# A 128-column stationary operand in one column stage of a four-layer convolution kernel on one Trainium2 core

## The chip, the cores and the metric

The kernel runs on one core of a Trainium2 chip. The metric is device time in microseconds (us) of one execution, everything on the chip included. An engine is named as in the profile: PE is TensorE (matmul), PEld its weight load, DVE is VectorE, ACT ScalarE, POOL GpSimd, and SP the queue that issues the DMAs.

## The reference, cut to what matters

Four layers act on `x` of shape (4, 64, 256, 256) in fp32. Layers 0, 2 and 3 are long convolutions; layer 1 goes to a Haar basis, mixes channels there, shrinks, and goes back.

```python
x = conv(x, L0)          # per channel: rows and columns convolved with a separable filter
f1 = haar2d(x)           # L1
acc = sum(soft_threshold(einsum('bchw,oc->bohw', f1 * v[i], conv_w[i]), tau[i]) for i in range(2))
x = haar2d(acc, inverse=True) + x
x = conv(x, L2)
x = conv(x, L3)

def conv(x, w):          # hx, hy: small sine networks of z, times a decay
    k = einsum('ijk,imk->ijmk', hx, hy)
    y = irfft2(rfft2(x, s=(512, 512)) * rfft2(k, s=(512, 512)) / 512)[..., :256, :256]
    return y + x * bias[:, None, None]
```

Since the filter of a channel is an outer product of two sequences, a convolution is a causal 256 by 256 Toeplitz product along the columns of an image and one along its rows.

## The kernel before, in words

**Tiles.** The four batches make two groups of two. A group has 32 rounds, and a round takes two channels of the two batches, so four images of 256 by 256. In SBUF the partition is (batch, 64 rows) and the free axis is (channel, block of 64 rows, column). There are 64 rounds, called t in the code; `alone` is 32, so t below 32 is the first group.

**Phases.** Phase A (t over all rounds) does layer 0 and the forward Haar. Phase B, once for each group, does the channel mix and the shrink in units: one unit is a matmul group `mix` (L607, four matmuls of 512 columns into the PSUM tile f), a multiply, subtract and threshold on DVE (L626, L646, L651), sign and magnitude on ACT, and additions on POOL (L669, L670). Phase C does the inverse Haar and layers 2 and 3.

**Phase C.** A round is 18 pieces, written out by hand in `piece`: four pieces of `rows` of layer 2 for t (PSUM tile c1r), a half of the inverse Haar product (c0ps, L308), four pieces of `columns` of layer 3 for t - 2 (c2c), four of `rows` of layer 3 for t - 1 (c2r), the other half of the Haar product, and four of `columns` of layer 2 for t (c1c). What a piece hands to ACT or DVE is queued with `later` and issued at the start of the next piece by `flush`. So each engine's order is fixed in the program.

**The Toeplitz product.** One piece is one j, a block of 64 output positions: `toeplitz` (the matmuls are L296) goes over four blocks k and, for each, over the four 64 by 64 tiles (r, c) of the PE array. The stationary operand is 64 by 64 of the data, the moving operand is the filter, 256 - 64k columns wide. A fp32 matmul is two passes, each with a weight load and a matmul in the profile. In the row stage r is the batch and c the channel; the result in PSUM has the channel on its partition half. ACT copies it to the SBUF tile `ch` (L861), after which a partition half is a channel. In the column stage r is the channel and c the batch; the filter, `filters_y(toep)`, depends on r alone. DVE adds the residual out of PSUM (`residual`, L880), into o for layer 3.

**What runs beside what.** `beside` interleaves lists of pieces by count. The mix of the second group (`phase_b(1)`) is spread over the first 29 rounds of phase C:

```python
cut_a, cut_c = (ROUNDS + 2) * A_PIECES + BLOCKS + 4, (ROUNDS - AHEAD) * C_PIECES
...
beside(main, phase_b(1), len(a_end) - 1 + 2 * BLOCKS, 0)
...
beside(c[cut_c:], [], 0, 0)
```

These rounds are called the shared stretch here; after them phase C runs by itself, the lone stretch. The column stage of layer 3 for t = 0 to 26 lies in the shared stretch, for t = 27 to 31 (and all of the second group) in the lone one.

Of the kernel before, what the change touches and what calls it, by code (L numbers as in the profile page):

```python
# [48 lines left out]
B, C, N = 4, 64, 256  # L49

ROW = 64
BLOCKS = N // ROW
# [46 lines left out]
def conv_haar_kernel(  # L99
    ctx: ExitStack, tc: tile.TileContext, x, zT, w1, wbd, cols, wo, decay, wo_first, decay_first, bias, forward, inverse, wrow, pack, v, v_rows, out  # L100
):
    nc = tc.nc
# [21 lines left out]
    def big(tag, name, bufs):  # L124
        return ac.tile([P, 2 * M, N], F32, tag=tag, name=name, bufs=bufs)

    def blocks(images):

        return images.rearrange("p (i k) j -> p i k j", i=2)
# [4 lines left out]
    def banks(name):  # L134

        ring = rings[asked[0] % len(rings)]
        asked[0] += 1
        return [ring.tile([P, 2, N], F32, tag="ps", name=f"{name}_{r}") for r in range(2)]
# [150 lines left out]
    def half(r):  # L289
        return slice(r * ROW, (r + 1) * ROW)  # L290

    def toeplitz(ps, data, t, j):

        for k in range(BLOCKS):
            for r, c in TILES:
                nc.tensor.matmul(  # L296
                    ps[r][half(c), j % 2, k * ROW :],
                    data[half(r), c, k, bass.ts(j, ROW)],
                    t(r, c)[:, : N - k * ROW],
                    start=k == 0,  # L300
                    stop=k == BLOCKS - 1,
                    tile_position=(r * ROW, c * ROW),
                )

    def haar(ps, pairs, matrix):

        for r, c in TILES:
            nc.tensor.matmul(  # L308
                ps[r][half(c)].rearrange("p h k -> p (h k)"),
                matrix[half(r)],  # L310
                pairs(r, c).rearrange("p h k -> p (h k)"),
                start=True,
                stop=True,
                tile_position=(r * ROW, c * ROW),
            )

    def filters_x(toep):
        return lambda r, c: toep[half(r), c * PERIOD : c * PERIOD + N]

    def filters_y(toep):  # L320
        return lambda r, c: toep[half(r), CI * PERIOD :]
# [72 lines left out]
    def later(op):  # L394

        waiting.append(op)
# [23 lines left out]
    def phase_a():  # L420
# [13 lines left out]
        def rows(t, j):  # L434
            s = st[t]
            if j == 0:
                s["y"] = big("t0", f"ay_{t}", 2)
            if j % 2 == 0:
                s["ps"] = banks(f"a1ps{j}_{t}")
            toeplitz(s["ps"], blocks(s["x"]), filters_x(s["toep"]), j)  # L440
            if j % 2:
                for r, ps in enumerate(s["ps"]):
                    y = blocks(s["y"])[:, r, j - 1 : j + 1]
                    later(lambda y=y, ps=ps: nc.scalar.copy(y, ps))  # L444

        def columns(t, j):
            s = st[t]
            if j == 0:
                s["x1"] = big("m0", f"x1_{t}", 2)
            if j % 2 == 0:  # L450
                s["ps2"] = banks(f"a2ps{j}_{t}")
            toeplitz(s["ps2"], blocks(s["y"]), filters_y(s["toep"]), j)
            if j % 2:
                for e, ps in enumerate(s["ps2"]):
                    later(lambda e=e, ps=ps: residual(t, e, j, ps))
            if j == BLOCKS - 1:
                s["fw"] = big("m1", f"fw_{t}", 2)
                s["ops"] = forward_free(s["x1"], s["fw"], f"f{t}_")
# [281 lines left out]
    def phase_c():  # L740
# [3 lines left out]
        alone = total - ROUNDS  # L744
# [3 lines left out]
        def load(t, k=slice(0, 4)):  # L748
            if t >= total:
                return  # L750
            if t < 2:
                g = bp.tile([P, 2, 2, W], F32, tag="v", name=f"g_{t}", bufs=3)
                st[t]["g"] = g.rearrange("p i k w -> p (i k w)").rearrange("p (n k) -> p n k", k=N)
            elif k.start == 0:
                st[t]["g"] = big("in", f"g_{t}", 3)
                st[t]["scales"] = scales(st[t]["g"])
            for rows, g in all_rows(mixed[t // ROUNDS], t % ROUNDS, st[t]["g"], False)[k]:
                nc.sync.dma_start(g, rows)

        def load_raw(t):  # L760
            if alone <= t < total:
                r = st[t]["raw"] = late["sb"].tile([P, 2 * M, N], F32, tag="raw", name=f"raw_{t}", bufs=2)
                for rows, to in all_rows(unshrunk, t % ROUNDS, r, False):
                    nc.sync.dma_start(to, rows)
# [71 lines left out]
        def product(t, h):  # L836
# [9 lines left out]
            for e, ps in enumerate(two):  # L846
                z = blocks(s["y"])[:, e, 2 * h : 2 * h + 2]
                copy = nc.vector.tensor_copy if e and t >= alone else nc.scalar.copy
                later(lambda z=z, ps=ps, copy=copy: copy(z, ps))

        def rows(t, l, j):
            s = st[t]
            if j == 0:
                s["half", l] = big("t0", f"ch{l}_{t}", 2)
            if j % 2 == 0:
                s["ps", l] = banks(f"c{l}r{j}_{t}")
            toeplitz(s["ps", l], blocks(s["y"]), filters_x(s["toep", l]), j)
            if j % 2:
                for r, ps in enumerate(s["ps", l]):
                    y = blocks(s["half", l])[:, r, j - 1 : j + 1]  # L860
                    later(lambda y=y, ps=ps: nc.scalar.copy(y, ps))  # L861

        def columns(t, l, j):
            s = st[t]
            if j == 0:
                s["new"] = big("out", f"o_{t}", 2) if l == 2 else big("m0", f"cy_{t}", 2)
            if j % 2 == 0:
                s["ps", l] = banks(f"c{l}c{j}_{t}")
            toeplitz(s["ps", l], blocks(s["half", l]), filters_y(s["toep", l]), j)
            if j % 2:  # L870
                new, old = blocks(s["new"]), blocks(s["y"])
                for e, ps in enumerate(s["ps", l]):
                    later(lambda e=e, ps=ps: residual(t, l, e, j, new, old, ps))
            if j == BLOCKS - 1:
                s["y"] = s["new"]

        def residual(t, l, e, j, new, old, ps):
            at = l * C + t % ROUNDS * CI + e
            to, of = new[:, e, j - 1 : j + 1], old[:, e, j - 1 : j + 1]
            nc.vector.scalar_tensor_tensor(to, of, bias_sb[:, at : at + 1], ps, ALU.mult, ALU.add)  # L880
            if l == 2 and t == total - 1:

                nc.sync.dma_start(blocks(out[t // ROUNDS, t % ROUNDS])[:, e, j - 1 : j + 1], to)
# [13 lines left out]
        def piece(t, j):  # L897
# [28 lines left out]
            if R1 <= j < R1 + BLOCKS:  # L926
                if t < total:
                    rows(t, 1, j - R1)
            elif C2 <= j < C2 + BLOCKS:
                if 1 < t:  # L930
                    columns(t - 2, 2, j - C2)
            elif R2 <= j < R2 + BLOCKS:
                if 0 < t <= total:
                    rows(t - 1, 2, j - R2)
            elif j >= C1:
                if t < total:
                    columns(t, 1, j - C1)
            else:
                product(t + 1, int(j > BLOCKS))
# [35 lines left out]

    late = {}
    (a, a_last, a_end), (c_before, c_first, c) = phase_a(), phase_c()

    cut_a, cut_c = (ROUNDS + 2) * A_PIECES + BLOCKS + 4, (ROUNDS - AHEAD) * C_PIECES
# [150 lines left out]
```

## Time and profile before

| | |
|---|---|
| median of 6 runs | 2567.8 us (2562.58 to 2578.39) |
| the profiled execution's own time | 2568.21 us |
| its span, first to last instruction | 2565.5 us |
| mean granted PE clock | 0.979 |
| PE busy | 2320.4 us (90%) |
| PEld busy | 1880.6 us (73%) |
| POOL busy | 2068.3 us (81%) |
| DVE busy | 1830.5 us (71%) |
| ACT busy | 1324.6 us (52%) |
| matmul group of the last column stage, c2c (L296) | 8192 passes, 319.1 us busy, 299 ns mean of one |
| first and last c2c matmul | 1169.4 us, 2561.0 us |

Times inside the span are counted from its first instruction. The end of a matmul is modelled, and it includes the time that results take to leave the array, so matmuls that follow each other overlap in the records, and a busy PE is not a PE at its peak. A matmul group's busy time counts overlapping ones once. A wait is put down to the instruction whose semaphore came last; "issue" means that the engine waited for nothing that the profile shows.

### The profile page before, as it was taken

The page shows a single profiled execution, that of the slowest core. Times are in us where ns is not written, and L with a number is a line of the kernel's source. Part 1 is how long each engine was busy: PE and PEld are TensorE (multiplying, and loading weights), DVE is VectorE, ACT ScalarE, POOL GpSimd, SP SyncE. Part 2 cuts the span into 40 slices and gives each one's busy share as a digit, 9 for nine tenths or more (in the row PEclk, how much of TensorE's full clock was granted, in tenths as well). Part 3 has the DMA queues.
Part 4 walks back from the last instruction along what each step waited for, and adds up shares of the span by engine and source line. Part 5 has one row for each costly group of instructions (what it writes and reads, how often), then busy time and mean ns, then how long its engine had stood idle before and what let it go on. Part 6 is the DMA issues. An engine that isn't in the chain of part 4 may idle for free.

```text
span 2565.5 us, 118462 instructions
## 1 busy us (share of the span) xinstructions
PE 2320.4 (90%) x53292; PEld 1880.6 (73%) x53292; DVE 1830.5 (71%) x2049; ACT 1324.6 (52%) x2187; POOL 2068.3 (81%) x2428
## 2 busy tenths in 40 slices
PE   5999998788888888878999999999989999999999
PEld 4877887445444444646777887777789999999998
DVE  2555545799999999856767676766757777777763
ACT  1221112566666666325666666666655555555552
POOL 1898887899989999768767777776879999999991
PEclk8999999899999999978999999999999999999999
DMA  7676998699999999656989898988876666666653
GB/s 211 223 246 229 295 310 294 249 346 319 339 341 314 351 322 328 239 194 207 325 306 315 310 327 308 310 308 300 293 224 220 216 209 221 215 212 215 219 163 110
DMA packets 203676, 685.23 MB, mean 267 GB/s; under 512 B 29289, under 2 KB 30826, under 8 KB 190755
## 3 DMA queue, kind: packets, MB, share of 16 engines
q1 hardware_dynamic: 203171, 677.67, 77.4%
q8 instruction: 418, 6.85, 1.1%
q14 instruction: 87, 0.71, 0.1%
HBM read 427.93 MB, written 249.63 MB: 264 GB/s over the span
## 4 chain that ended last, share of the span: by engine, by line
PE 47%; DVE 4%; issue 2%; DMA 1%; POOL 1%; ACT 1%; SPq 0%; DVEq 0%; ACTq 0%; POOLq 0%
PE c2c L296 10%; PE c2r L296 10%; PE c1r L296 10%; PE c1c L296 9%; PE f L607 4%; PE c0ps L308 4%; DVE cy L880 1%; DVE m L651 1%; DVE x L626 1%; DVE x L646 1%; DMA ft<-coef 0%; POOL i L385 0%; DMA toep<-filt 0%; DMA rows<-in_v_rows 0%; ACT ch L861 0%
## 5 line engine op out<-in xcount | busy, mean ns | idle before, releaser
L385 POOL TENSOR_TENSOR i<-i,g 128x16 f32<-128x16 f32 x744 | 431.6, 600 | 27.2
L296 PEld LDWEIGHTS a2ps<-toep,ay 64*64 64x64 f32 x8192 | 306.4, 137 | 146.8 <-DVE f L477 71.8
L607 PE MATMUL f<-ft,mix 64*64 64x512 f32 x2048 | 301.9, 620 | 110.7 <-DVE x L626 89.5
L296 PE MATMUL a2ps<-toep,ay 64*64 64x128 f32 (+3 forms) x8192 | 356.6, 307 | 33.3 <-DVE f L477 28.5
L296 PEld LDWEIGHTS a1ps<-toep,x 64*64 64x64 f32 x8192 | 288.4, 134 | 87.8 <-issue 45.9
L296 PE MATMUL a1ps<-toep,x 64*64 64x128 f32 (+3 forms) x8192 | 336.3, 299 | 16.2 <-DMA x<-in_x 9.9
L296 PEld LDWEIGHTS c2c<-toep,ch 64*64 64x64 f32 x8192 | 311.9, 134 | 46.6 <-issue 17.2
L296 PEld LDWEIGHTS c1c<-toep,ch 64*64 64x64 f32 x8192 | 302.3, 133 | 47.0 <-issue 20.1
L296 PE MATMUL c1r<-toep,z 64*64 64x256 f32 (+3 forms) x8192 | 320.4, 299 | 12.8 <-issue 8.5
L296 PEld LDWEIGHTS c1r<-toep,z 64*64 64x64 f32 x8192 | 299.5, 134 | 42.4 <-issue 25.4
L296 PE MATMUL c2c<-toep,ch 64*64 64x128 f32 (+3 forms) x8192 | 319.1, 299 | 8.1 <-ACT ch L861 5.4
L385 POOL TENSOR_TENSOR ci<-i,g 128x1024 f32<-128x1024 f32 x124 | 317.3, 2579 | 4.5
L296 PEld LDWEIGHTS c2r<-toep,cy 64*64 64x64 f32 x8192 | 296.8, 134 | 32.3 <-issue 21.3
L296 PE MATMUL c2r<-toep,cy 64*64 64x128 f32 (+3 forms) x8192 | 314.0, 298 | 6.0 <-issue 4.4
L669 POOL TENSOR_TENSOR gt<-m,ft 128x512 f32<-128x512 f32 x128 | 163.3, 1276 | 193.2 <-DVE m L651 189.7
L296 PE MATMUL c1c<-toep,ch 64*64 64x256 f32 (+3 forms) x8192 | 311.8, 297 | 4.8 <-issue 3.5
L444 ACT COPY ay<-a1ps 128x512 f32<-128x512 f32 x256 | 137.3, 589 | 346.0 <-PE a1ps L296 345.4
L632 ACT ACTIVATE m<-x 128x1024 f32<-128x1024 f32 x194 | 206.0, 1062 | 210.2 <-DVE x L626 102.2
L861 ACT COPY ch<-c2r 128x512 f32<-128x512 f32 x256 | 137.3, 590 | 291.2 <-PE c2r L296 290.5
L477 DVE TENSOR_TENSOR f<-a3ps,wrow_sb 128x512 f32<-128x512 f32 x256 | 161.3, 681 | 132.9 <-PE a3ps L308 132.9
L626 DVE TENSOR_TENSOR x<-f,v 128x1024 f32<-128x1024 f32 x192 | 233.1, 1214 | 20.5 <-PE f L607 19.4
L880 DVE SCALAR_TENSOR_TENSOR o<-cy,bias_sb,c2c 128x512 f32<-128x512 f32 x256 | 176.7, 740 | 95.4 <-PE c2c L296 94.9
(84 smaller groups left out, 3941.3 us busy)
## 6 DMA issues: line engine op xcount, KB each, us to landing
toep<-filt SPq DMA_DIRECT2D x384, 224.0 KB, 5.1
ft<-coef SPq DMA_DIRECT2D x128, 512.0 KB, 7.9
v<-in_v SPq DMA_DIRECT2D x64, 1024.0 KB, 9.1
mixed<-gt SPq DMA_DIRECT2D x128, 512.0 KB, 6.9
g<-mixed SPq DMA_DIRECT2D x256, 256.0 KB, 5.0
x<-in_x SPq DMA_DIRECT2D x128, 256.0 KB, 4.4
coef<-f SPq DMA_DIRECT2D x128, 256.0 KB, 3.8
x<-in_x SPq DMA_DIRECT2D x32, 1024.0 KB, 8.1
```

The lines of the kernel that those rows point to most:

```text
L296: nc.tensor.matmul(ps[r][half(c), j % 2, k * ROW :], data[half(r), c, k, bass.ts(j, ROW)], t(r, c)[:, : N - k * ROW], start=k == 0, stop=k ...
L308: nc.tensor.matmul(ps[r][half(c)].rearrange("p h k -> p (h k)"), matrix[half(r)], pairs(r, c).rearrange("p h k -> p (h k)"), start=True, s ...
L385: engine.tensor_tensor(to, s, d, op)
L444: later(lambda y=y, ps=ps: nc.scalar.copy(y, ps))
L477: later(lambda f=f, ps=ps, w=w: nc.vector.tensor_tensor(f, ps, w, ALU.mult))
L607: nc.tensor.matmul(un[u]["f4"][half(q), b, :], mixers[0][half(r), bass.ts(i, C)], st[s]["f"][half(r), b], start=True, stop=True, tile_posi ...
L626: nc.vector.tensor_tensor(un[u]["x"], un[u]["f4"], both(u, "v"), ALU.mult)
L632: nc.scalar.activation(un[u]["m"], un[u]["x"], AF.Sign)
L646: nc.vector.tensor_tensor(un[u]["a"], un[u]["a"], both(u, "tau"), ALU.subtract)
L669: nc.gpsimd.tensor_tensor(g[:, 0], m[:, 0], st[s]["f"][:, 0], ALU.add)
L861: later(lambda y=y, ps=ps: nc.scalar.copy(y, ps))
L880: nc.vector.scalar_tensor_tensor(to, of, bias_sb[:, at : at + 1], ps, ALU.mult, ALU.add)
```

## The change

In the column stage of layer 3 for the first group, `wide(t, l)`, the two images of one channel (the two batches) are multiplied in one stationary operand of 64 partitions by 128 columns, on the 64 by 128 half r of the array, instead of two operands of 64 by 64. So that the 128 columns lie next to each other, ACT writes the row results `ch` in the order (k, j, image, 64) instead of (image, k, 256); `turn` does it, in as many copies as before. Each j has 8 matmuls instead of 16, with moving operands of the same widths. In the built program the PE has 1024 c2c matmuls of 64 by 128 in place of 2048 of 64 by 64, out of 4096; the orders of ACT, DVE, POOL and SP stay as they were, but for the shape of 128 copies. `mix` pieces and the other stages keep 64 by 64 tiles, so the wide matmuls stand in 54 unbroken runs, 49 in the shared stretch and 5 in the lone one.

```diff
+    def side_by_side(data):
+
+        return data.rearrange("p n k -> p (n k)").rearrange("p (k j c q) -> p k j c q", k=BLOCKS, j=BLOCKS, c=2)
+
+    def toeplitz_wide(ps, data, t, j):
+
+        for k in range(BLOCKS):
+            for r in range(2):
+                nc.tensor.matmul(
+                    ps[r][:, j % 2, k * ROW :],
+                    data[half(r), k, j].rearrange("p c q -> p (c q)"),
+                    t(r, 0)[:, : N - k * ROW],
+                    start=k == 0,
+                    stop=k == BLOCKS - 1,
+                    tile_position=(r * ROW, 0),
+                )
+
+    def turn(data, r, j, ps):
+
+        to = side_by_side(data)[:, j - 1 : j + 1, :, r]
+        nc.scalar.copy(to, ps.rearrange("p i (j q) -> p i j q", q=ROW))
...
+        def wide(t, l):
+            return t < alone and l == 2
+
         def rows(t, l, j):
...
                 for r, ps in enumerate(s["ps", l]):
+                    if wide(t, l):
+                        later(lambda r=r, ps=ps: turn(s["half", l], r, j, ps))
+                        continue
                     y = blocks(s["half", l])[:, r, j - 1 : j + 1]
                     later(lambda y=y, ps=ps: nc.scalar.copy(y, ps))
...
-            toeplitz(s["ps", l], blocks(s["half", l]), filters_y(s["toep", l]), j)
+            if wide(t, l):
+                toeplitz_wide(s["ps", l], side_by_side(s["half", l]), filters_y(s["toep", l]), j)
+            else:
+                toeplitz(s["ps", l], blocks(s["half", l]), filters_y(s["toep", l]), j)
```

## The prediction

> **What bounds the kernel now.** The page's chain comes first: it tells whose time the end is made of. PE leads by far, and its part is spread evenly over the six Toeplitz stages, c2c with a tenth.
>
> ```profile
> PE 47%; DVE 4%; issue 2%; DMA 1%; POOL 1%; ACT 1%; SPq 0%; DVEq 0%; ACTq 0%; POOLq 0%
> ```
>
> Then the two stretches in which the changed stage runs, by windows cut at starts of c2c stages: 25 rounds of the shared stretch, 20 of the lone one. The columns are length, busy time of each engine with its records, PE clock, DMA share and GB/s.
>
> ```profile
> core 0: us, PE busy (x) PEld busy (x) DVE busy (x) ACT busy (x) POOL busy (x), PEclk, DMA share, GB/s
> 1206.50:1851.20 644.70, 607.08 (x14152) 499.58 (x14148) 453.26 (x434) 405.64 (x709) 465.57 (x519) 1.00 0.90 312
> 1918.90:2303.30 384.40, 384.28 (x10568) 368.71 (x10563) 283.39 (x320) 224.30 (x421) 362.38 (x361) 1.00 0.67 215
> ```
>
> In the lone stretch PE never stops: 384.40 / 20 = 19.2 us a round. In the shared one a round takes 644.7 / 25 = 25.8 us, PE is busy for 94%, and DVE, ACT and POOL for 63 to 72%. So PE sets the pace in both, and what the change does to PE counts. How near it is to its peak shows in one row for each width of the moving operand, here in the lone stretch (busy, then mean ns of one):
>
> ```profile
> L296 PE MATMUL c2c<-toep,ch 64*64 64x256 f32 x160 | 17.4, 377 | 0.0
> L296 PE MATMUL c2c<-toep,ch 64*64 64x192 f32 x160 | 15.2, 323 | 0.0
> L296 PE MATMUL c2c<-toep,ch 64*64 64x128 f32 x160 | 13.1, 269 | 0.0
> L296 PE MATMUL c2c<-toep,ch 64*64 64x64 f32 x160 | 11.0, 217 | 0.0
> ```
>
> Sixty-four columns more cost 53 ns (377 - 323, and so on down), so a pass streams 1.2 columns per ns, and 217 - 53 = 164 ns of each record is the way out of the array. A j has two passes at each of the four widths on each tile: 2 x (213 + 160 + 107 + 53) = 1.07 us if the four tiles stream side by side. Four stages of four j give 17.1 us, and two Haar products (512 columns, two passes: 0.85 each) 1.7, together 18.8 of the 19.2 us. The array is full with 64 by 64 tiles. The wide form has half the matmuls on half the tiles, so it streams for the same 1.07 us; it has nothing to win in the stream, and the question is what comes between the streams.
>
> **Part 1, weight loads.** A load of 64 columns against one of 128, from the c2c loads and from the network's product in phase A (min/median/max):
>
> ```profile
> L296 PEld LDWEIGHTS c2c<-toep,ch x640: 130/133/136, 2206.9 to 2288.6; 64*64 64x64 f32 x160
> L195 PEld LDWEIGHTS mlp_ps<-h,wbd_sb x4: 186/190/190, 98.8 to 99.3; 128*128 128x128 f32 x4
> ```
>
> The difference is 190 - 133 = 57, about 54 ns for 64 columns: a load takes its columns at 1.2 per ns too, 53 and 107 ns. In the records a tile's next load begins as its present matmul begins and runs below it, so a pass costs the longer of its stream and the next load. With 53 ns that hides below every width; 107 ns stands out by 53 ns below the 64-column passes, two in each j. That is 107 ns for a j, 4 x 32 = 128 of them: 13.7 us. In each of the 54 runs the last such pass has no wide load behind it: less 54 x 0.053 = 2.9. Part 1 costs 10.8 us, 9.0 in the shared stretch and 1.8 in the lone one.
>
> The Trainium skill (TensorE: Matmul & The Clock Gate, What overlaps and what doesn't) says that a weight load overlaps running matmuls only in other row groups. By that rule each of the 32 loads of a row half in a stage would stand bare, 32 x 32 x 0.107 = 110 us in all, by estimate; the product at 98.8 us, with all 128 rows in use, contradicts it, since its loads of 107 ns lie below streams of 213 ns and add nothing.
>
> **Part 2, changing the shape of the tile.** Before, phase C has one shape. Afterwards each run is entered and left. The nearest rows are in phase A, where a 128 by 128 product stands between 64 by 64 ones:
>
> ```profile
> 98.65 0.22 PE L296 MATMUL a2ps<-toep,ay 64*64 64x64 f32 x1
> 98.79 0.73 PEld L195 LDWEIGHTS mlp_ps<-h,wbd_sb 128*128 128x128 f32 x4
> 98.79 1.13 PE L195 MATMUL mlp_ps<-h,wbd_sb 128*128 128x256 f32 x4
> 99.85 0.45 PE L296 MATMUL a1ps<-toep,x 64*64 64x256 f32 x4
> ```
>
> The last narrow stream ends at 98.65 + 0.05 = 98.70, and the first load of the new shape starts only at 98.79: 94 ns in which nothing may begin, and then 107 ns of load. Four streams of 0.213 end at 99.75; the next load comes at 99.85, again 94 ns on, with 53 ns to fill. In and out cost 0.20 + 0.15 = 0.35 us. The other changes of shape in phase A (into and out of mlp_out, of 128 rows by 64 columns) show 90 to 97 ns as well. 54 runs x 0.35 = 18.9 us: 17.1 shared, 1.8 lone. All of these rows also change the number of rows, 64 to 128; the new change, 64 by 64 to 64 by 128, alters only the columns. So the bounds are 0 and 18.9 us (and 2 more, since the four tiles end up to 57 ns apart and wait for the last). I take 18.9, as every change of shape in the trace shows it.
>
> The Trainium skill (TensorEngine Tiling (Array Packing), Key Properties) states that a change of tiling mode, not of tile alone, drains the engine, and lists 64 by 64 and 64 by 128 as different configurations: by that rule the upper bound holds, without it the sum below would be about zero.
>
> **Part 3, fewer instructions.** PE's unexplained idle time in the shared stretch (us in total, times, longest):
>
> ```profile
> PE c1r L296 <- issue: 7.0, 10, 1.7
> PE c2r L296 <- issue: 4.4, 5, 1.4
> PE c1c L296 <- issue: 3.5, 5, 1.5
> PE f L607 <- issue: 2.9, 4, 1.1
> PE c2c L296 <- issue: 2.5, 3, 1.9
> ```
>
> With c0ps (0.3) it is 20.6 us in 28 stops, or 25 from the end of the streams (28 x 0.164 more). Number the PE and PEld records in order of time, and these stops begin at numbers that leave 193 or 194 over 256. The page has the partner:
>
> ```profile
> q8 instruction: 418, 6.85, 1.1%
> ```
>
> The 53292 matmul and 53918 load records over 418 packets are 256 a packet: PE waits for its next packet of instructions, in the stretch where the DMA share is 0.90. The lone stretch, at 0.67, has no such stop. The shared window has 28300 records, 110 packets, so 0.23 us a packet. The change takes 256 records out of each of 27 rounds, one packet: 27 x 0.23 = 6.2 us. The packet that lies in the wide stage also lasts up to twice as long, which gives the fetch time; I take half of another 6.2. Relief 9 us; bounds 0 and 25.
>
> The Trainium skill (Runtime: NRT & Kernel Launch, Instruction fetch mechanics) calls the crossing of such a block mostly hidden. By that rule the relief would be nothing and the sum 9 us higher; the 25 us above speak against it for this stretch.
>
> **Part 4, what absorbs it.** Other stops of PE in the shared stretch are mostly mix waiting for DVE to free its PSUM tile (9.4 us) and shape no steady limit; a longer c2c shortens some: 3 us (0 to 6). At the start of the lone stretch PE waits on the rows' DMA anyway, so t = 27 is free: 0.7 us. The ACT copies keep size and place in the order, 588 ns each; they write 64 elements at a time, which no row prices, but ACT is busy 63% of the shared stretch, and `ch` is read most of a round later. At nothing then; if each took half as long again, 128 x 0.29 = 38 us of ACT work would spread over 670 us with 37% idle. No wait, DMA or queue place is added on any engine.
>
> **Sum.** 10.8 + 18.9 - 9 - 3 - 0.7 = 17 us on the profiled execution's 2568.2, which is 0.4 above the median: 2585 us. With all bounds for slower (no relief, nothing absorbed, 2 us for uneven ends) it is + 32; with no drain, + 13.7 - 9 - 3.7 = + 1.
>
> **Rivals.** *No measurable change.* Either only the row split counts for the drain, which gives 2569, or the relief is nearer 20 than 9, which gives 2574. For it: no row shows this very change of shape, and the stops feed back on pace. Against: 94 ns in every change that is shown. *Faster.* The missing packet lets the fetch run ahead, so that all 25 us of stops go, and there is no drain: 13.7 - 25 = - 11, with the 6 us of other waits - 17, so 2551 us. It decides where the relief passes the sum of parts 1 and 2; if part 2 holds, at 30 us, it can't be reached. *Much slower.* The two row halves don't stream side by side in this shape; then a stage takes 4.27 us longer, 32 x 4.27 = 137 us, and with 9 us of relief the time is near 2695. Against: in the 64 by 64 shape the same two halves do run together; no row has two wide tiles. (The Trainium skill, TensorE: Matmul & The Clock Gate, Measured speedup vs the span model, has four row tiles at 3.07 times one; no run here shows it.) That the change isn't made is excluded: the built program has 1024 matmuls of 64 by 128.
>
> **How the numbers follow.** Forecast (slower by 13 to 32 us) 0.57, much slower 0.08, no measurable change 0.25, faster 0.10. About 0.5%, 12.8 us, is what a measurement of this kernel can tell. Slower is 0.57 + 0.08. The likeliest case alone spans 2581 to 2600. The range goes down to 2566 to take in the undrained case, and up to 2601; it leaves out faster, much slower, and a little beyond the bounds.
>
> **What would show it.** In the profile after: a c2c load of about 187 ns, 64 columns; the first load of a wide run 94 ns after the last stream; a j of 1.17 us inside a run; in the lone stretch 20.0 us a round for t = 28 to 31 against 19.2; fewer "issue" stops in the shared stretch. Streams of the two halves that alternate, or a run entered without a gap, would prove it wrong.

## The result, and the profile after

The changed kernel takes 2578.83 us (median of 23 runs, 2573.41 to 2587.25) against 2570.7 us for the kernel before, run beside it (53 runs). The ratio is 1.0033, 95% interval 1.0023 to 1.0043: about 8.5 us slower, clear of the noise, and half of the 17 us that the sum gave. The time lies in the stated range, but below the likeliest case (13 to 32 us slower), and 8.5 us is less than the 12.8 us (0.5%) that the prediction took for the least that can be told; with this many runs it can be told.

The profiled execution has a span of 2578.1 us, 12.6 more than the one before. Of these, 7.3 us have passed when the first c2c matmul starts, before any wide matmul. They are put down to the spread between executions: in the profiles of all kernels below the first c2c load starts between 1168.9 and 1175.1 us without wide stages and between 1167.4 and 1179.3 us with them. The rest follows from the starts of the c2c stages. The 25 shared rounds between the same two stages take 648.1 us against 644.6, so 3.5 more; the kernel that is wide in all rounds, which has the same program in this stretch, takes 647.2, so a difference of 1 us between single profiles means nothing. The rounds t = 29 to 31 of the lone stretch take 59.7 us against 57.6, so 2.1 more for three; the remainder of the kernel is the same to 0.3 us.

The windows of the changed kernel, shared and lone:

```profile
core 0: us, PE busy (x) PEld busy (x) DVE busy (x) ACT busy (x) POOL busy (x), PEclk, DMA share, GB/s
1213.90:1862.00 648.10, 622.28 (x12550) 476.41 (x12546) 457.38 (x434) 405.78 (x709) 463.35 (x519) 0.99 0.89 310
1930.30:1990.00 59.70, 59.70 (x1396) 49.86 (x1396) 44.06 (x48) 33.78 (x64) 54.34 (x55) 1.00 0.64 206
```

The same three lone rounds of the kernel before:

```profile
1918.90:1976.50 57.60, 57.60 (x1592) 55.12 (x1588) 42.84 (x48) 33.97 (x64) 54.81 (x55) 1.00 0.65 211
```

The shared stretch has 12550 + 12546 matmul and load records in place of 28300, so 128 fewer in each of 25 rounds. One lone round is 0.7 us longer (59.7 / 3 = 19.9 us). The wide stage itself, t = 30, by the width of the moving operand (busy, mean), with all wide loads of the run below (min/median/max):

```profile
L313 PE MATMUL c2c<-toep,ch 64*128 64x256 f32 x16 | 2.7, 410 | 0.0
L313 PE MATMUL c2c<-toep,ch 64*128 64x192 f32 x16 | 2.0, 322 | 0.0
L313 PE MATMUL c2c<-toep,ch 64*128 64x128 f32 x16 | 1.6, 271 | 0.0
L313 PE MATMUL c2c<-toep,ch 64*128 64x64 f32 x14 | 1.2, 241 | 0.0
L313 PEld LDWEIGHTS c2c<-toep,ch x2048: 182/187/335, 1176.7 to 1974.9; 64*128 64x128 f32 x187
```

A load takes 187 ns, as the 128-column loads of phase A did. The 192- and 128-column passes keep their 322 and 271 ns. Half of the 64-column ones wait for the next load (241 ns on average against 217), and so does the first pass of the next j. The two halves stream together: their matmuls start 7 ns apart. A j takes 1.20 us. The entry and the way out of that run:

```profile
1949.29 1.04 PE L330 MATMUL c0ps<-ci,inverse_sb 64*64 64x512 f32 x8
1950.26 0.52 PEld L313 LDWEIGHTS c2c<-toep,ch 64*128 64x128 f32 x6 [0.81 <-issue]
1950.26 0.70 PE L313 MATMUL c2c<-toep,ch 64*128 64x256 f32 x4
...
1954.19 1.10 PE L313 MATMUL c2c<-toep,ch 64*128 64x256 f32 x14
1955.22 0.80 PEld L296 LDWEIGHTS c2r<-toep,cy 64*64 64x64 f32 x20
```

The Haar product's modelled end is 1949.29 + 1.04 = 1950.33; less the 164 ns way out, its streams end at 1950.17, and the first wide load starts at 1950.26. In 53 of the 54 entries this gap is 89 to 92 ns; in one it is 560. On the way out the last wide stream ends at 1954.19 + 1.10 - 0.164 = 1955.13, and the first narrow load starts at 1955.22, about 90 ns on as well. The waits of PE in the shared stretch, of the changed kernel:

```profile
PE f L629 <- DVE x L648: 16.1, 19, 2.8
PE c1r L296 <- issue: 3.7, 7, 1.7
...
PE c1c L296 <- issue: 1.7, 2, 1.5
...
PE c2c L313 <- issue: 0.4, 1, 0.4
```

The stops for no shown reason are 5.8 us in 10, against 20.6 us in 28 before. Those of `mix` for DVE have grown; before, the row was:

```profile
PE f L607 <- DVE x L626: 9.4, 13, 1.4
```

### The profile page after: what moved, and what is told of

It reads as the page before. It is cut to its first block, busy times and chain, and to the rows that moved or that the text cites. A ratio compares the mean times of both kernels' runs of the same rounds, so it can differ in the third digit from the quotient of the medians.

```text
span 2578.1 us, 114366 instructions
## 1 busy us (share of the span) xinstructions
PE 2340.7 (91%) x51244; PEld 1825.9 (71%) x51244; DVE 1833.0 (71%) x2049; ACT 1324.4 (51%) x2187; POOL 2067.1 (80%) x2428
## 4 chain that ended last, share of the span: by engine, by line
PE 43%; DVE 6%; DMA 2%; issue 2%; POOL 2%; ACT 2%; SPq 0%; DVEq 0%; ACTq 0%; POOLq 0%
PE c2r L296 9%; PE c1r L296 9%; PE c1c L296 8%; PE c2c L296 5%; PE c2c L313 5%; PE c0ps L330 4%; PE f L629 3%; DVE m L673 1%; DVE cy L911 1%; DVE x L668 1%; DVE x L648 1%; DMA mixed<-gt 1%; POOL i L407 1%; DVE o L911 0%; ACT ch L325 0%
## 5 line engine op out<-in xcount | busy, mean ns | idle before, releaser
L296 PE MATMUL a2ps<-toep,ay 64*64 64x192 f32 (+3 forms) x8192 | 355.1, 305 | 36.0 <-DVE f L499 29.6
L296 PE MATMUL a1ps<-toep,x 64*64 64x192 f32 (+3 forms) x8192 | 338.5, 300 | 18.4 <-DMA x<-in_x 13.7
L296 PEld LDWEIGHTS c1c<-toep,ch 64*64 64x64 f32 x8192 | 280.2, 133 | 62.9 <-issue 37.1
L296 PEld LDWEIGHTS c1r<-toep,z 64*64 64x64 f32 x8192 | 285.9, 136 | 45.8 <-issue 20.1
L296 PEld LDWEIGHTS c2r<-toep,cy 64*64 64x64 f32 x8192 | 273.9, 134 | 41.5 <-issue 18.6
L296 PE MATMUL c2r<-toep,cy 64*64 64x256 f32 (+3 forms) x8192 | 301.1, 298 | 2.1 <-DMA toep<-filt 2.1
L296 PE MATMUL c1c<-toep,ch 64*64 64x256 f32 (+3 forms) x8192 | 298.8, 297 | 1.7 <-issue 1.7
L366 POOL TENSOR_TENSOR fw<-x 128x1024 f32<-128x1024 f32 x64 | 122.5, 1915 | 142.1 <-DVE x L486 138.5
L889 ACT COPY ch<-c1r 128x512 f32<-128x512 f32 x256 | 137.9, 594 | 191.3 <-PE c1r L296 190.9
L486 DVE SCALAR_TENSOR_TENSOR x<-x,bias_sb,a2ps 128x512 f32<-128x512 f32 x256 | 179.3, 742 | 79.4 <-PE a2ps L296 60.2
```

The costliest lines, as they stand in the source:

```text
L296: nc.tensor.matmul(ps[r][half(c), j % 2, k * ROW :], data[half(r), c, k, bass.ts(j, ROW)], t(r, c)[:, : N - k * ROW], start=k == 0, stop=k ...
L486: nc.vector.scalar_tensor_tensor(to, old, bias_sb[:, c : c + 1], ps, ALU.mult, ALU.add)
```

## The experiments

All compare with the kernel before on the same chip. In the text a stream is the time that a pass takes for its columns at 1.2 per ns from its record's start, and a gap is time in which none streams. Such gaps include short ones that the wait rows leave out. The columns are the ratio with its interval, the 25 shared rounds of the profile, their matmul and load records over 256 (packets), the stops that the profile calls "issue", and the waits of `mix` for DVE.

| kernel | ratio | shared us | packets | issue us | mix <- DVE us |
|---|---|---|---|---|---|
| before | 1 | 644.6 | 110.5 | 20.6 | 11.2 |
| changed | 1.0033 [1.0023, 1.0043] | 648.1 | 98.0 | 5.8 | 16.1 |
| wide in all 64 rounds | 1.0121 [1.0101, 1.0141] | 647.2 | 98.0 | 5.5 | 18.4 |
| before, fewer loads | 0.9921 [0.9904, 0.9939] | 624.7 | 110.5 | 0 | 31.0 |
| changed, fewer loads | 1.0035 [1.0022, 1.0048] | 649.8 | 98.0 | 0 | 30.7 |
| both column stages wide | 1.0050 [1.0032, 1.0068] | 653.1 | 85.5 | 0 | 12.0 |
| before, one run | 0.9995 [0.9979, 1.0012] | 648.4 | 110.5 | 18.7 | 21.5 |
| changed, one run | 1.0033 [1.0019, 1.0046] | 650.4 | 98.0 | 4.9 | 27.0 |
| shared only, one run | 1.0021 [1.0007, 1.0035] | 654.4 | 98.0 | 5.0 | 27.6 |
| both stages, one run | 1.0050 [1.0031, 1.0070] | 655.5 | 85.5 | 1.4 | 24.0 |
| c2c cut finer | 1.0156 [1.0123, 1.0189] | 682.6 | 123.0 | 53.3 | 8.3 |
| all four stages cut finer | 1.0799 [1.0763, 1.0834] | 839.9 | 160.5 | 166.3 | 1.2 |

**The price without any relief: wide in all rounds.**

```diff
         def wide(t, l):
-            return t < alone and l == 2
+            return l == 2
```

> The last column stage is wide for all 64 rounds, so 32 more stages, all in the lone stretch, 86 runs of wide matmuls in place of 54. Theory (each run costs 0.35 us to enter and leave, each j 0.107 us of weight load, and the lone stretch has no instruction stop to give back): 32 x 0.78 = 25 us above the changed kernel, about 33 above the kernel before, ratio 1.013. Rival (the costs of parts 1 and 2 are half of what was reckoned, and that is why the change cost only 8 us): 12 us above the changed kernel, ratio 1.008.

The time is 1.0121 - 1.0033 = 0.9% above the changed kernel, 22.6 us by medians of ratios. In its profile the kernel after the start of stage t = 31 takes 632.4 us against 607.9 in the changed one: 24.5 us for 32 stages, 0.77 each. The sizes of parts 1 and 2 hold where PE has nothing to win back; the rival's half price doesn't.

**Are the stops instructions that queue behind data? Fewer loads.** The same edit in both kernels: the second group's mix uses the coefficients of its first 4 steps and the v and tau of its first 3 for all later ones.

```diff
+            if grp and s >= 4:
+                d["f"] = kept["f", s % 4]
+                return
+            kept["f", s] = d["f"] = bp.tile(
...
+            if grp and s >= 3:
+                d["v"], d["tau"] = kept["v", s % 3]
+                return
```

> The kernel before, but the second group's mix loads its coefficients only for the first 4 steps and v and tau only for the first 3 and uses these again, which takes about 2.4 MB a round off the DMA queues in the shared stretch. Theory (PE's stops at every 256th instruction come from its instruction packets queueing behind data on busy DMA engines): DMA share of the shared stretch falls from 0.90 to under 0.70, the stops there from 31 us to under 10, and the time by 20 to 30 us, ratio 0.990. Rival (the stops don't depend on the load of the DMA engines, or other waits take their place): stops and time as before, ratio 0.997 to 1.

> The changed kernel with the same loads left out as in the kernel before with fewer loads. Theory (the change costs PE some 24 us in the shared stretch and wins back 20 of them in instruction stops): with the stops gone beforehand there is nothing to win back, so this kernel is 22 to 28 us slower than the kernel before with fewer loads, not 8. Rival (the 24 us were absorbed by waits for DVE and other engines): the difference stays at 8 us.

The shared window of the kernel before with fewer loads, and its largest wait of PE:

```profile
1207.30:1832.00 624.70, 593.66 (x14148) 474.49 (x14144) 461.33 (x434) 405.92 (x708) 476.32 (x519) 0.99 0.64 224
PE f L614 <- DVE x L633: 25.7, 22, 3.0
```

The same of the changed kernel with fewer loads:

```profile
1204.60:1854.40 649.80, 619.08 (x12550) 470.83 (x12546) 459.93 (x434) 405.89 (x709) 462.54 (x519) 0.99 0.62 215
PE f L636 <- DVE x L655: 26.3, 21, 3.2
```

With the DMA share at 0.64 and as many instructions as before, no "issue" stop is left, and the kernel is 0.79% faster; 20 us of the shared stretch are gone. The 0.997 to 1 of the rival is excluded. The changed kernel gains nothing from fewer loads, so the two now stand 2577.81 - 2550.59 = 27.2 us apart in place of 8, and 25.1 us in the shared stretch, against the 24.2 that parts 1 and 2 give for 25 rounds ((9.0 + 17.1) x 25 / 27). That is the theory's 22 to 28, and not the rival's 8. What hid two thirds of the cost in the changed kernel is the stops. One thing goes with it: in both kernels `mix` waits some 15 to 20 us more for DVE, so taking stops away frees less than their whole length.

The trace's own records of the instruction packets (queue q8) show the link. One packet stands for each 256 instructions of PE, its sequencer's counted too. None of the 112 in the shared stretch of the kernel before is begun by PE sooner than 1.24 us after it has landed, and all 35 stops longer than 150 ns at a 256th record, the 28 of the wait rows among them, end 1.24 to 1.60 us after a landing. A packet itself takes 1.0 to 1.1 us (median) in either stretch. But in this one it starts 2.7 us (median) after PE has begun the packet before it, against 0.9 in the lone stretch, and 0.9 in the shared stretch with fewer loads. So what goes with the busy DMA engines is a late start of the packet, not a slow transfer.

**More wide stages.**

```diff
         def wide(t, l):
-            return t < alone and l == 2
+            return t < alone and l > 0
```

> The column stages of layers 2 and 3 are both wide for the first group: 105 runs in place of 54, 128 more j. PE gains 51 x 0.30 + 128 x 0.107 = 29 us more. Theory (about 11 us of instruction stops are left in the shared stretch to win back): 18 to 25 us above the changed kernel, ratio to the kernel before 1.011. Rival (slack of other waits absorbs two thirds of what PE gains): 8 to 10 us above the changed kernel, ratio 1.007.

Neither. The ratio is 1.0050, so 4 us above the changed kernel, with intervals that overlap; I had expected 18 to 25 from the theory, and the rival 8 to 10. Counted from the ends of the streams, gaps at and inside wide runs rise from 26.1 to 48.2 us in the shared stretch, as costed. But the stops fall from 11.2 to 2.9 (those too short for the profile's wait rows counted), and the gaps in front of `mix` from 19.5 to 12.9. With 2.2 less in the streams and small gaps that is the 5.0 us of difference in the shared stretch. So, by these single profiles, slack in front of `mix` does absorb PE time when the work is spread, and the theory that stops alone do it was too narrow.

**Fewer, longer runs.** Weights of zero keep pieces of the second group's mix out of the wide stage.

```diff
-    beside(main, phase_b(1), len(a_end) - 1 + 2 * BLOCKS, 0)
+    at = 2 * BLOCKS + len(a_end) - 1 + mid - BLOCKS
+    weights = [int((k - at) % C_PIECES not in (BLOCKS + 1, BLOCKS + 2, BLOCKS + 3)) for k in range(C_PIECES)]
+    beside(main, phase_b(1), len(a_end) - 1 + 2 * BLOCKS, 0, weights)
```

> The kernel before, but the pieces of the second group's mix are kept out of the last column stage (weights of zero for three of its four pieces) and spread over the other 15 pieces of a round. It is the control for the next kernels. Both theories: within 4 us of the kernel before, ratio 0.999 to 1.002.

> The changed kernel with the mix kept out of the wide stage: 32 unbroken runs in place of 54. Theory (0.35 us a run, of which 0.05 are weight load that comes back in the j): 22 x 0.30 = 6.6 us below the changed kernel, so about 2 us above the kernel before, ratio 1.001. Rival (entering and leaving a run costs little, since PE would have waited for the mix's PSUM tile there anyway): no gain over the changed kernel, ratio 1.0033.

The control is where it was expected, and the changed kernel gained nothing. The change of shape does cost less: gaps on entering and leaving fall from 13.8 to 6.0 us in the shared stretch. But the gaps in front of `mix` rise from 19.5 to 34.8. The wait rows show it, first of the control, then of the changed kernel with one run:

```profile
PE f L607 <- DVE x L626: 21.1, 22, 2.4
```

```profile
PE f L629 <- DVE x L648: 26.7, 21, 3.9
```

Before the bunching they were 9.4 and 16.1 us. The rival's result came, though for another reason than it named: not that a change of shape in front of `mix` is free, but that units of the mix closer together wait for DVE. The edit mixes two things, and only the gaps tell them apart.

Two more kernels on this line, the second with zero weights for both stages and both wide up to their last shared round:

```diff
-            return t < alone and l == 2
+            return t < alone - AHEAD - 2 and l == 2
```

> As the one before, and wide only for t below 27, so only in the shared stretch: 27 runs. Theory: another 4 to 5 stages at 0.72 to 0.78 us less, about 3 us, so 1 us below the kernel before, ratio 0.9995. Rival: 5 us above the kernel before, ratio 1.002.

> Both column stages wide in the shared stretch alone, the mix kept out of both: 56 runs in place of 105. Theory: 49 x 0.30 = 15 us for the runs and 8 x 0.72 = 6 us for the stages of the lone stretch below the kernel with both column stages wide (12 us above the kernel before), so about 8 us below the kernel before, ratio 0.997. Rival (with the mix bunched into 12 of 18 pieces PE waits longer for DVE between its units, which takes this back): ratio 1.000 to 1.005.

The first is 0.12% below the changed kernel with one run: 3 us, the size expected for the stages of the lone stretch, though the two intervals overlap. In its profile the rounds t = 28 to 31 are back at 19.6 us each, from 20.2. But the base had gained nothing. The second is 1.0050 in place of 0.997: the bunched mix takes back what 49 fewer runs and the lone stages save. No wide version here beats the kernel before.

**The number of instructions by itself.** These go the other way, on the kernel before, with 64 by 64 tiles throughout: each matmul of k = 1 and 2 is cut in two halves of its moving operand. The streams are the same in sum, and the number of passes goes up by half.

```diff
+        for k in range(BLOCKS):
+            n = N - k * ROW
+            parts = 2 if k in (1, 2) else 1
+            for q in range(parts):
+                at = slice(q * n // parts, (q + 1) * n // parts)
...
+                        ps[r][half(c), j % 2, k * ROW + at.start : k * ROW + at.stop],
...
+                        t(r, c)[:, at],
...
-            toeplitz(s["ps", l], blocks(s["half", l]), filters_y(s["toep", l]), j)
+            (toeplitz_split if t < alone and l == 2 else toeplitz)(s["ps", l], blocks(s["half", l]), filters_y(s["toep", l]), j)
```

> The kernel before with 64 by 64 tiles, but in the last column stage of the first group the moving operands of k = 1 and k = 2 (192 and 128 columns) are cut in two halves, each with a matmul of its own: 96 matmuls a stage in place of 64, so 128 more matmul and load records, half an instruction packet more a round. All streams (96 and 64 columns) still cover a load of 64 columns, so the array has the same work; the lone stretch shows whether it does. Theory (a packet crossed in the shared stretch costs 0.28 us of stop, more where it is used up faster): 4 to 12 us slower, ratio 1.0015 to 1.005, all in the shared stretch. Rival (the number of instructions plays no part in PE's stops): no change, ratio 0.999 to 1.001.

> The same cut in all four Toeplitz stages of phase C for the first group: 512 more records a round, 2 packets more in 4.4. A packet then lasts 2.9 us inside a stage in place of 4.4, while its fetch takes 1 us after its turn in the queue. Theory: 15 to 50 us slower, ratio 1.006 to 1.02, with the stops at every 256th record in the shared stretch at 50 us or more (31 before), and next to nothing in the lone rounds. Rival: no change, ratio 0.999 to 1.002.

The waits of PE in the shared stretch, first with c2c cut, then with all four stages cut:

```profile
PE c2c L313 <- issue: 24.2, 19, 3.0
PE c2r L296 <- issue: 15.5, 11, 3.5
```

```profile
PE c1c L313 <- issue: 54.1, 32, 3.8
PE c1r L313 <- issue: 38.9, 27, 3.0
PE c2c L313 <- issue: 37.9, 22, 3.8
PE c2r L313 <- issue: 22.9, 15, 3.5
```

The direction is the theory's and the rival is out, but the size was missed by factors: 40 us in place of 4 to 12, and 206 in place of 15 to 50. With c2c cut, the shared stretch is 38.0 us longer; gaps at every 256th record, short ones counted, rise from 31.2 to 67.5 us, 36.3 of the 38. The cut isn't wholly free in the lone stretch: a round is 1.3 us longer, of which 0.8 are gaps (most of them at a 256th record, with a DMA share of 0.63) and about 0.4 are not explained; in the shared one that leaves little unexplained.

With all four stages cut, two things were not as expected. Here are its shared stretch and its rounds t = 28 to 30 of the lone one, then the same three rounds of the kernel before:

```profile
1212.60:2052.50 839.90, 669.11 (x20551) 552.71 (x20547) 426.82 (x434) 406.04 (x708) 443.97 (x527) 0.95 0.71 242
2109.60:2184.30 74.70, 63.75 (x2166) 56.67 (x2162) 43.79 (x45) 34.31 (x65) 50.81 (x52) 0.98 0.50 160
```

```profile
1898.00:1957.30 59.30, 58.22 (x1589) 55.30 (x1584) 43.31 (x47) 36.27 (x67) 54.82 (x55) 1.00 0.64 210
```

First, the lone rounds were to lose next to nothing, and they take 15.4 us more for three, of which 13.1 are gaps at a 256th record, at a DMA share of 0.50. So a high DMA share is not needed for the stops: PE gets through 256 records in as little as 2.8 us there, against 4.2 in the kernel before. Second, the shared stretch is 195 us longer, and its gaps at a 256th record grow by only 156 of them, from 31 to 187. The granted clock was at half for about 85 us of this stretch, against 4 before, which by estimate is worth up to 41 us. No run separates this part from the number of instructions.

The five kernels with data loads in full and the mix spread lie on one rising curve. At 85.5, 98.0, 110.5, 123.0 and 160.5 packets the stops are 0, 5.8, 20.6, 53.3 and 166.3 us. Between the second and third it is 1.2 us a packet, between the third and fourth 2.6, after that 3.0. Most packets cost nothing and some cost a microsecond or more; the mean of 0.2 us describes neither. How fast the packet before is used up plays a part, but doesn't decide alone: of the 56 packets used up fastest in the shared stretch of the kernel before 22 are followed by a stop, of the other 56 it is 13.

## Why the prediction was right, and where it was not

**What held.** The direction and what PE pays. That the time lies in the range owes something to luck: the part of the range below 2581 us was put in for a change of shape that costs nothing, and the profile rules that out. The time came to lie there because part 3 was mis-sized. *Part 1:* a load of 187 ns that stands out below the 64-column passes; a j of 1.20 us against 1.17 forecast. *Part 2:* 89 to 92 ns in which nothing begins on entry, in a change from 64 by 64 to 64 by 128, which no row of before had shown. The bound of 0 is excluded. Together 0.7 us a stage in the lone stretch as costed (0.72), confirmed 32 times over by the kernel that is wide in all rounds (0.77). *Much slower* is out: the two halves stream side by side.

**What failed: part 3, in both factors.** The count was wrong. A wide stage has 128 records fewer, half a packet and not one, as the windows after show (28300 to 25096 records in 25 rounds). (The 53918 "load records" are 53292 loads and 626 instructions of PE's sequencer; the packets hold these too, so the 256 stand.) The price was wrong by more: a mean of 0.23 us over all packets was taken, where most packets cost nothing and the ones at the margin cost 1.2 by the wait rows. Counting short stops too, gaps at every 256th record fell from 31.2 to 11.2 us: a relief of 20, not 9. The second, "nearer 20 than 9, which gives 2574", had been set down under *no measurable change*, with a chance of 0.25; the measured time lies between that and the forecast.

**Part 4** had the wrong sign: the waits of `mix` for DVE didn't shrink by 3 us but grew by 5 in the profile's rows. The start of the lone stretch did swallow the first stage, as the same time between the starts of t = 26 and t = 28 shows (46.8 us before, 46.9 after). The ACT copies, put at nothing, took 588 ns as before.

**The account of the shared stretch**, from the gaps between streams: wide runs + 26.1, stops - 20.0, gaps in front of `mix` + 2.5, other gaps - 0.4, streams - 4.7 (594.4 to 589.7 us; probably the ragged ends around stops, for with fewer loads, where the stops are gone, the streams take 584.1 us with narrow tiles and 586.0 with wide ones), together + 3.5. With 0.7 a round for the four lone stages that count, about 6 us; the measured 8.5 has an interval of 5.9 to 11.1.

**The two rules.** The Trainium skill's rule that a change of tiling mode drains the engine (TensorEngine Tiling (Array Packing), Key Properties) fits part 2: 89 to 92 ns in 53 of 54 entries. The Trainium skill's rule that crossing an instruction block is mostly hidden (Runtime: NRT & Kernel Launch, Instruction fetch mechanics) fits the kernel before where its DMA share is 0.67, with no stop, and 0.64 with fewer loads. It does not fit the shared stretch at 0.90, with 20.6 us of stops in 28, nor the kernel with all four stages cut finer, which stops at shares of 0.71 and 0.50 too.

## What to carry to other kernels

Price a change in the number of instructions at the margin: see whether the engine stops at packet boundaries, and in which stretch, before taking a mean. A change that makes one engine's work longer can still come out nearly even if it gives the same engine back a stop, so test it with that stop taken away by other means; here that turned 8 us into 27. Beside a chain that waits for another engine, moving work together to save one cost may lose it in the wait.

## What was not expected of the hardware

Half as many PE instructions again in the four Toeplitz stages of the first group, with the array's streams the same in sum, made the whole kernel 8% slower. Most of it is stops at every 256th instruction: 156 of 195 us in the shared stretch, at a DMA share of 0.71, and 13.1 of 15.4 us in three lone rounds, at 0.50. The granted PE clock of the shared stretch fell to 0.95 from 1.00 as well, and no run tells whether the stops brought that about.
